# Three vector instructions moved at the hand-over from self-attention to cross-attention, in a fused stack of attention layers

## The chip, the cores and the metric

The kernel runs on one core of a Trainium2 chip. Such a core has a matrix engine (TensorE, PE in the profile, with its weight loads as PEld) and three others that work on vectors: VectorE (DVE), ScalarE (ACT) and GpSimd (POOL). A fifth queue, SyncE (SP), issues transfers. Each engine takes its instructions in the order of its own queue; between engines, semaphores make one wait for another. Matmuls read from the on-chip memory SBUF and write to the accumulators, PSUM, which POOL doesn't use here.

The metric is the device time of one execution in microseconds, as the median of several runs.

## What is computed

Four blocks one after another, on x of shape (8, 256, 128) and a context of shape (8, 64, 64), in float32. The third block is nearly all of the work: six layers, each with self-attention (16 heads of 64, a mask on the keys), cross-attention to the context's 64 rows (16 heads, a mask), and a feed-forward part. Cut to what matters:

```python
def _mha(s, t, kv_w, q_w, o_w, o_b, mask):
    kv = s @ kv_w
    k, v = jnp.split(kv, 2, axis=-1)
    q = t @ q_w
    k, v, q = (_heads(k), _heads(v), _heads(q))
    scores = jnp.einsum('bhqd,bhkd->bhqk', q, k) * D ** (-0.5)
    scores = jnp.where(mask[:, None] == 0, jnp.float32(-1000000000.0), scores)
    attn = jax.nn.softmax(scores, axis=-1)
    o = jnp.einsum('bhqk,bhkd->bhqd', attn, v)
    o = o.transpose(0, 2, 1, 3).reshape(t.shape[0], t.shape[1], H * D)
    return o @ o_w + o_b

def step(t, p):
    skv, sq, sow, sob, ckv, cq, cow, cob, w1, b1, w2, b2, pg, pb = p
    tn = _ln(t, norm_g, norm_b)
    t = _mha(tn, tn, skv, sq, sow, sob, tgt_mask) + t
    tn = _ln(t, norm_g, norm_b)
    t = _mha(src, tn, ckv, cq, cow, cob, src_mask) + t
    tn = _ln(t, pg, pb)
    t = t + (jax.nn.relu(tn @ w1 + b1) @ w2 + b2)
    return (t, None)
```

Two smaller attention blocks come ahead of the six layers and one behind them.

## The kernel before

**An order written by hand.** The program is laid out in *ticks*. `at(tick, phase, fn)` (L304) puts a step down; at the end the steps are run sorted by tick and then by phase, and each engine's instructions are chained in just that order (L1338 to L1348). So the phase of a step is its place in the queue of every engine that it uses; a step with instructions on ACT, DVE and POOL takes a place in all three. Transfers (SP) aren't chained. Between engines only data and free buffers make an instruction wait.

**A layer.** Self-attention (`plan_sa`) takes four ticks a batch, for eight batches; cross-attention (`plan_ca`) then takes two ticks a batch, one for each tile of 128 query rows (`qt`). With `T_ca` as the first tick of cross-attention, the hand-over is:

- tick `T_ca - 2`, phase 3.7: `keys_both` makes the keys of batches 0 and 1 (matmuls L1138, copies to SBUF on ACT, L1144).
- tick `T_ca - 1`: the last two score tiles of self-attention (batch 7). `scores` (L946, PE), `exps` (L960 on DVE: mask, minimum and copy out of PSUM; L965 on ACT: exponential and its sum), `divide` (reciprocal L973 on DVE, four scalings L975 on POOL), `turn` (two 32 x 32 block transposes L985 on DVE). The first tile's `divide` is at phase 2.3 and its `turn` at 8.1; the second's `divide` is at 8.0 and its `turn` at phase 2.2 of tick `T_ca`. At phase 3.0 stand the attention sums of the first half of the heads (`values(0)`, L1001), whose two PSUM tiles are copied out by L309 (DVE) and L311 (ACT). At phase 6 stand the next batch's moments for the layer norm (L856 to L862, DVE).
- tick `T_ca`: `scores` of cross-attention for batch 0, first query tile (L366, PE, phase 1), and `lower` (phase 2): the copy out of PSUM (L377, ACT), the maximum of each row and head (L379, DVE), its subtraction (L380, POOL). At phase 8 the exponential (L386, ACT).
- tick `T_ca + 1`: the same for the second query tile; `divide` of the first (sums L390 and reciprocal L391 on DVE, scaling L392 on POOL) at phase 2.4; `values(1)`, the attention sums that need the last `turn`, at phase 3.0 (L1001, copies L309 and L311).
- tick `T_ca + 2`: `scores` for batch 1 (L366), a pair of transposes (L889), the output projection of batch 7's self-attention (L1019), the context's values for batch 0 (L328, copied by L334 on ACT), the keys of batches 2 and 3 (L1138).

**The mask of the context's keys.** `mask_keys` (L1150) adds a row of the mask to the last 32 partitions of a batch's keys, in place: one instruction of 32 x 1024 elements with two inputs in SBUF (L1152). Queries have a constant in their last row, so the scores get the mask with the matmul. It stands at phase 1.9 of tick `T - 1` for even batches and `T - 2` for odd ones, where `T` is the batch's first tick: for batch 0 that is `T_ca - 1`, for batch 1 it is `T_ca`, ahead of `lower`.

**PSUM.** One pool of four tiles of two banks serves every matmul in turn, so a tile is written again only when the fourth one back has been copied out. The tile of L1019 is the one that L309 empties for `values(1)`.

Of the kernel before, what the change touches and what calls it, by code (L numbers as in the profile page):

```python
# [27 lines left out]
def tile_xattn_stack(ctx: ExitStack, tc: tile.TileContext, io, out: bass.AP):  # L28
    nc = tc.nc
# [15 lines left out]
    def two_banks(base):  # L45
        return psum.tile([P, 1024], F32, tag="ps", name=uniq(base))
# [10 lines left out]
    def big(tag, bufs=4, shape=(P, 1024), dtype=F32):  # L57

        return heap.tile(list(shape), dtype, tag=tag, name=uniq(tag), bufs=bufs)
# [244 lines left out]
    def at(tick, phase, fn):  # L304
        plan.setdefault(tick, []).append((phase, fn))
# [7 lines left out]
    def residual(b, bias):  # L313
        tb = sb([P, QT, D], "tb", 3)
        nc.gpsimd.tensor_tensor(
            tb, tt(b), bias.unsqueeze(1).to_broadcast([P, QT, D]), ALU.add
        )
        return tb

    def values_of(b, wvo):  # L320

        ps = two_banks("mm").rearrange("p (r k x) -> p r k x", r=2, k=2)
        w = wvo.rearrange("p (g a) d -> p a g d", g=2)
        for k in range(2):
            for a in range(4):
                for r in range(2):
                    rows = slice(r * DM, (r + 1) * DM)
                    nc.tensor.matmul(  # L328
                        ps[32 * a : 32 * a + 32, r, k, :],
                        lhsT=ctx2[rows, b, 32 * k : 32 * k + 32],  # L330
                        rhs=w[rows, a], start=True, stop=True,
                    )
        vw = big("v", shape=(P, 2, 2, 2, D))
        nc.scalar.copy(  # L334
            vw.rearrange("p r k g d -> p (r k g d)"), ps.rearrange("p r k x -> p (r k x)")
        )
        return vw

    def plan_weights_64(tick, qt, qT, keys, values, halves, take):

# [95 lines left out]
            take(ps)  # L438

        at(tick, 1, scores)  # L440
        at(tick, 2, lower)
        if halves:
            at(tick + 1, 2.05, exps)
            at(tick + 1, 2.5, turn)
# [245 lines left out]
    def plan_l0(b, T):  # L690
# [88 lines left out]
        for qt in range(QT):  # L779
            plan_weights_64(  # L780
                T + qt, qt, lambda: st["q"], lambda: st["k"], lambda: st["VW"], True,
                lambda ps, qt=qt: add(qt, ps),
            )
# [342 lines left out]
    def plan_ca(l, b, T):  # L1126
        st = {}
        fold = W["fold", l]

        def keys_both():  # L1130

            res = [big("q", shape=(D, 4, 4, M)) for _ in range(2)]
            for g in range(2):
                ps = two_banks("mm").rearrange("p (r a x) -> p r a x", r=2, a=4)
                for a in range(4):
                    for r in range(2):
                        rows = slice(r * DM, (r + 1) * DM)
                        nc.tensor.matmul(  # L1138
                            ps[:, r, a, :], lhsT=fold["AT"][rows, 4 * g + a, :],
                            rhs=ctx2[rows, b : b + 2, :].rearrange("p b m -> p (b m)"),  # L1140
                            start=True, stop=True,
                        )
                for i in range(2):
                    nc.scalar.copy(  # L1144
                        res[i][:, :, 2 * g : 2 * g + 2, :].rearrange("p a r k -> p r a k"),
                        ps[:, :, :, i * M : (i + 1) * M],
                    )
            keys_of[b], keys_of[b + 1] = res

        def mask_keys():  # L1150
            last = keys_of[b][96:].rearrange("p a c k -> p (a c) k")
            nc.vector.tensor_tensor(  # L1152
                last, last, nm2[96:, b].unsqueeze(1).to_broadcast([32, 16, M]), ALU.add
            )

        def make_values():
            st["VW"] = values_of(b, fold["WVO"])

        def res():
            st["tb"] = residual(b, W["ca", l][3])  # L1160

        ahead(b, (T - 5, 6), (T - 3, 2.95), (T - 2, 2.9), last_off, last_on, st)
        if b % 2 == 0:
            at(T - 2, 3.7, keys_both)
        at(T - 1 - b % 2, 1.9, mask_keys)
        at(T + 2, 3.2, make_values)
        at(T + 2, 7, res)

        def add(qt, ps):
            nc.vector.tensor_add(t[:, QT * b + qt, :], ps[:, :D], st["tb"][:, qt, :])  # L1170

        for qt in range(QT):
            plan_weights_64(
                T + qt, qt, lambda: st["tT"], lambda: keys_of[b], lambda: st["VW"],
                False, lambda ps, qt=qt: add(qt, ps),
            )

    def plan_ff(l, b, T, T_second, steps=None):
# [117 lines left out]
    for l in range(NL):  # L1296
        T_ca = T0 + 4 * B
        T_next = T_ca + 2 * B
        for b in range(B):
            plan_sa(l, b, T0 + 4 * b)  # L1300
        plan_ca_weights(l, T_ca - 7)
        for b in range(B):
            plan_ca(l, b, T_ca + 2 * b)
            T_ff = T_ca + 2 * b + 7
            if l + 1 < NL:
                plan_ff(l, b, T_ff, T_ff + 2)
            elif b < B - 2:
                plan_ff(l, b, T_ff, T_ff + 1)
            else:

                T_ff -= b - B + 3
                done = T_ca + 2 * b + 4
                plan_ff(
                    l, b, T_ff, T_ff + 1,
                    (4.6, (done, 6), (done, 8.7), (T_ff, 2.9)),
                )
            T_end[b] = T_ff + 1
        if l > 0:
            at(T0 + 8, -1, lambda l=l: load_ff(l))
        if l + 1 < NL:  # L1320
            at(T_ca + 4, -1, lambda l=l: load_sa(l + 1))
            at(T_next + 1, -1, lambda l=l: load_ca(l + 1))
        T0 = T_next
# [82 lines left out]
```

## Time and profile before

| what | us |
|---|---|
| median of 3 runs | 2408.69 (2408.59 to 2411.47) |
| the profiled execution's own time | 2410.73 |
| its span (first to last instruction) | 2409.0 |
| one layer (from one layer's first L1152 to the next's) | 368.6 |
| L1152 on DVE, 48 in all | 1.22 to 1.65 each |
| L379 on DVE, 112 in all | 1.22 each |
| L380 on POOL, 112 in all | 1.90 each |
| L985 on DVE, 768 in all | 0.69 each |
| mean granted TensorE clock | 0.985 |

The page gives for each engine its busy time, its share of the span and its instructions. The chain of work that ended last is followed back from the last instruction, at each step to what released it. A timeline has a line for each run of like instructions: start, time, engine, line, operation, out<-in, shapes, count, and in brackets the idle time before it and what ended it. A table of stretches has, for each, its length, the busy time of an engine with its number of records, the TensorE clock that was granted (1.00 is full), the share of the DMA engines and GB/s. Times within the span count from its start.

On DVE, the hand-over of the first layer begins with the mask of batch 0 at 393.00 us, and the mask of batch 1 runs at 401.63.

### The profile page before, as it was taken

Reading aid. Unit: us, or ns where it says so; the run is one execution under the profiler, and the core shown is the slowest. Engines: PE = TensorE matmul, PEld = TensorE weight load, DVE = VectorE, ACT = ScalarE, POOL = GpSimd, SP = SyncE. Lnnn points to the kernel's source line nnn. Section 1 sums busy time; section 2 is a strip of 40 time slices with the busy share of each in tenths; the row PEclk is TensorE's granted clock in tenths of the full one; section 3 lists DMA queues with packets and bytes.
Section 4 is the critical chain, followed back from the end, with each engine's and each line's share of the span. In section 5 each row is a group of like instructions: output and inputs, shape, how many; then the busy total and the mean of one; then the engine's idle time right before and its main releaser. Section 6 shows DMA issues by size and latency. Waiting matters only on the chain.

```text
span 2409.0 us, 97481 instructions
## 1 busy us (share of the span) xinstructions
PE 2300.7 (96%) x41124; PEld 1696.1 (70%) x41124; DVE 1922.7 (80%) x6269; ACT 1720.0 (71%) x4544; POOL 1398.4 (58%) x2243
## 2 busy tenths in 40 slices
PE   7889999999998999998999999899999899999897
PEld 3557776777776777776677777677777677777675
DVE  5678888967888967888877888877888877888885
ACT  4567777767777677777677778677778668777663
POOL 2445556854555864555865555865555774555774
PEclk9989999999999999999999999999999999999998
DMA  6000012001012001012001012000012000010000
GB/s 180 2 12 15 21 56 65 2 3 30 21 50 60 12 3 30 21 43 68 12 3 30 21 38 71 14 2 18 25 38 73 21 2 18 25 38 12 2 4 16
DMA packets 98932, 70.67 MB, mean 29 GB/s; under 512 B 7936, under 2 KB 93632, under 8 KB 98496
## 3 DMA queue, kind: packets, MB, share of 16 engines
q1 hardware_dynamic: 97904, 64.12, 9.9%
q8 instruction: 323, 5.29, 1.0%
q14 instruction: 113, 0.93, 0.1%
q10 hardware_dynamic: 592, 0.33, 0.1%
HBM read 59.19 MB, written 5.24 MB: 27 GB/s over the span
## 4 chain that ended last, share of the span: by engine, by line
PE 80%; DVE 11%; ACT 6%; issue 1%; POOL 1%; DMA 1%; SPq 0%; ACTq 0%; POOLq 0%; DVEq 0%
PE mm L909 14%; PE sc L946 13%; PE mm L1001 13%; PE mm L1019 7%; PE mm L928 7%; PE mm L434 6%; PE sc L366 4%; PE mm L1203 4%; PE mm L1186 3%; DVE m L379 2%; PE mm L328 2%; DVE e L960 2%; PE tp L889 2%; ACT e L965 1%; PE mm L1138 1%
## 5 line engine op out<-in xcount | busy, mean ns | idle before, releaser
L975 POOL TENSOR_SCALAR e<-e,rs 128x256 f32<-128x256 f32 x1536 | 714.8, 485 | 724.7 <-DVE rs L973 714.8
L965 ACT ACTIVATE e<-e,mn 128x256 f32<-128x256 f32 x1536 | 758.5, 495 | 145.5 <-DVE mn L960 144.6
L960 DVE CUSTOM_DVE_ANT_0 e<-sc,nm 128x256 f32<-128x256 f32 x1536 | 543.4, 419 | 116.7 <-PE sc L946 115.3
L985 DVE STREAM_TRANSPOSE eTc<-e 128x512 f32<-128x512 f32 x768 | 513.8, 693 | 54.0 <-POOL e L975 53.1
L1001 PE MATMUL mm<-eTc,v 32*64 32x256 f32 x12288 | 372.7, 385 | 25.1 <-DVE eTc L985 25.1
L946 PE MATMUL sc<-k,q 64*32 64x256 f32 x12288 | 380.5, 382 | 1.4 <-ACT v L311 0.6
L1001 PEld LDWEIGHTS mm<-eTc,v 32*64 32x64 f32 x12288 | 283.8, 134 | 111.0 <-issue 44.3
L380 POOL TENSOR_TENSOR e<-e,m 128x1024 f32<-128x1024 f32 x112 | 213.1, 1902 | 207.1 <-DVE m L379 206.8
L946 PEld LDWEIGHTS sc<-k,q 64*32 64x32 f32 x12288 | 221.7, 107 | 122.9 <-issue 45.9
L965 ACT ACTIVATION_READ_ACCUMULATOR e<-e,mn 128x1 f32 x1536 | 287.7, 187 | 0.0
L379 DVE TENSOR_REDUCE m<-e 128x16 f32<-128x1024 f32 x112 | 136.4, 1218 | 102.4 <-ACT e L377 100.3
L434 PE MATMUL mm<-v,o 128*128 128x128 f32 x1536 | 192.8, 279 | 18.7 <-DVE o L400 11.5
L434 PEld LDWEIGHTS mm<-v,o 128*128 128x128 f32 x1536 | 178.9, 192 | 41.4 <-issue 26.9
L909 PE MATMUL mm<-tT,w_sk 128*128 128x256 f32 x768 | 189.3, 389 | 0.0
L1019 PEld LDWEIGHTS mm<-w_sow,o 128*128 128x128 f32 x1536 | 175.1, 192 | 19.0 <-issue 12.3
L311 ACT COPY v<-mm 128x1024 f32<-128x1024 f32 x96 | 97.2, 1012 | 124.8 <-PE mm L928 124.8
L1019 PE MATMUL mm<-w_sow,o 128*128 128x128 f32 x1536 | 183.6, 278 | 2.8 <-ACT WVO L1100 2.8
L366 PE MATMUL sc<-q,tT 128*32 128x256 f32 x3072 | 185.5, 382 | 0.3 <-DVE t L1170 0.3
L928 PE MATMUL mm<-w_sv,tT 128*32 128x256 f32 x3072 | 185.6, 382 | 0.0
L392 POOL TENSOR_TENSOR e<-e,r 128x1024 f32<-128x1024 f32 x96 | 182.6, 1902 | 0.5 <-DVE r L391 0.5
L909 PE MATMUL mm<-tT,w_sq 128*128 128x256 f32 x768 | 173.6, 379 | 0.0
L909 PEld LDWEIGHTS mm<-tT,w_sk 128*128 128x128 f32 x768 | 138.2, 190 | 44.2 <-issue 29.2
(226 smaller groups left out, 3457.6 us busy)
## 6 DMA issues: line engine op xcount, KB each, us to landing
nm<-mask_d SPq DMA_DIRECT2D x192, 128.0 KB
w_sk<-in_L_sa_kv_dram SPq DMA_DIRECT2D x6, 512.0 KB
w_sv<-in_L_sa_kv_dram SPq DMA_DIRECT2D x24, 128.0 KB
w_sq<-in_L_sa_q_dram SPq DMA_DIRECT2D x6, 512.0 KB
w_sow<-in_L_sa_ow_dram SPq DMA_DIRECT2D x6, 512.0 KB
w_ckv<-in_L_ca_kv_dram SPq DMA_DIRECT2D x12, 256.0 KB
w_cq<-in_L_ca_q_dram SPq DMA_DIRECT2D x6, 512.0 KB
w_cow<-in_L_ca_ow_dram SPq DMA_DIRECT2D x6, 512.0 KB
```

The lines of the kernel that those rows point to most:

```text
L366: nc.tensor.matmul(sc[32 * a : 32 * a + 32, q, :], lhsT=qT()[:, qb * 32 : (qb + 1) * 32], rhs=keys()[:, a].rearrange("p h k -> p (h k)"), ...
L380: nc.gpsimd.tensor_tensor(e, e, m.unsqueeze(2).to_broadcast([P, 16, M]), ALU.subtract)
L434: nc.tensor.matmul(ps[:, :D], lhsT=eT[:, s].rearrange("p q x -> p (q x)"), rhs=vw[:, r, k, g, :], start=(s == 0), stop=(s == 7),)
L909: nc.tensor.matmul(ps[:, i * S : (i + 1) * S], lhsT=w[:, c * P : (c + 1) * P], rhs=st["tT"], start=True, stop=True,)
L928: nc.tensor.matmul(ps[32 * a : 32 * a + 32, i, :], lhsT=st["tT"][:, kb * 32 : (kb + 1) * 32], rhs=sv[:, a].rearrange("p g x -> p (g x)"), ...
L946: nc.tensor.matmul(sc[32 * a : 32 * a + 32, r, j, :], lhsT=st["q"][g][rows, a, qb * 32 : (qb + 1) * 32], rhs=st["k"][g][rows, a, :], start ...
L960: nc.vector.tensor_tensor_reduce(e[:, i, :], sc4[:, i, :], st["nm"][:, 2 * jj + i % 2, :], -1.0, 3.0 * BIG, ALU.add, ALU.min, mn[:, i : i ...
L965: nc.scalar.activation(e[:, i, :], e[:, i, :], AF.Exp, scale=-1.0, bias=mn[:, i : i + 1], accum_out=rs[:, i : i + 1],)
L975: nc.gpsimd.tensor_scalar(e[:, i, :], e[:, i, :], rs[:, i : i + 1], 1.0, ALU.mult, ALU.mult)
L985: nc.vector.transpose(eT[:, r, :, 2 * jj : 2 * jj + 2, :], e[:, 2 * r : 2 * r + 2, :].rearrange("p j (k x) -> p k j x", x=32),)
L1001: nc.tensor.matmul(ops[a // 2][r * HD : (r + 1) * HD, a % 2, :S], lhsT=st["v"][kb // 4][rows, kb % 4, (2 * g + r) * HD : (2 * g + r + 1) * ...
L1019: nc.tensor.matmul(st["ps"][:, j * D : (j + 1) * D], lhsT=st["oT"][c // 4][:, c % 4, j * P : (j + 1) * P], rhs=sow[:, c, :], start=(c == 0 ...
```

## The change

`mask_keys` of batch 0 is issued on GpSimd, at phase 2.2 of tick `T_ca - 1` and not on VectorE at 1.9. That of batch 1 stays on VectorE and in tick `T_ca`, but moves from phase 1.9 to 5.5. The step `lower` of batch 0's first query tile moves from phase 2 to 2.25 of tick `T_ca`, which puts its three instructions behind the turning at 2.2. All other batches keep their places.

In the queues, for each of the six layers: POOL gets L1152 between the eight scalings L975 that were there and the next four. VectorE loses L1152 ahead of the last two score tiles. Further on, its order was L1152, L379, two L985, L379 and becomes two L985, L379, L1152, L379. TensorE's, ScalarE's and SyncE's orders stay as they were.

```diff
-    def plan_weights_64(tick, qt, qT, keys, values, halves, take):
+    def plan_weights_64(tick, qt, qT, keys, values, halves, take, lower_at=2):
...
         at(tick, 1, scores)
-        at(tick, 2, lower)
+        at(tick, lower_at, lower)
...
         def mask_keys():
             last = keys_of[b][96:].rearrange("p a c k -> p (a c) k")
-            nc.vector.tensor_tensor(
+            (nc.vector if b else nc.gpsimd).tensor_tensor(
                 last, last, nm2[96:, b].unsqueeze(1).to_broadcast([32, 16, M]), ALU.add
             )
...
         if b % 2 == 0:
             at(T - 2, 3.7, keys_both)
-        at(T - 1 - b % 2, 1.9, mask_keys)
+
+        at(T - 1 - b % 2, {0: 2.2, 1: 5.5}.get(b, 1.9), mask_keys)
         at(T + 2, 3.2, make_values)
...
             plan_weights_64(
                 T + qt, qt, lambda: st["tT"], lambda: keys_of[b], lambda: st["VW"],
                 False, lambda ps, qt=qt: add(qt, ps),
+                2.25 if b == 0 and qt == 0 else 2,
             )
```

## The prediction

> **What bounds the kernel now.** First the page's busy times and its chain of work that ended last:
>
> ```profile
> PE 2300.7 (96%) x41124; PEld 1696.1 (70%) x41124; DVE 1922.7 (80%) x6269; ACT 1720.0 (71%) x4544; POOL 1398.4 (58%) x2243
> PE 80%; DVE 11%; ACT 6%; issue 1%; POOL 1%; DMA 1%; SPq 0%; ACTq 0%; POOLq 0%; DVEq 0%
> ```
>
> TensorE sets the end nearly everywhere, so time is to be had only where it waits. The change acts once in each of six layers, where self-attention hands over to cross-attention. The first mask L1152 starts at 393.0, 761.6, 1130.1, 1498.7, 1867.2 and 2235.8 us, with the same neighbours each time, so I work out the first layer and multiply by six. The chain in order of time (start, us, what):
>
> ```profile
> 393.00 1.23 DVE q L1152
> ...
> 401.63 1.33 DVE q L1152
> 403.00 1.22 DVE m L379
> 404.21 0.63 DVE eTc L985
> ...
> 404.98 5.89 PE mm L1001 x128
> ```
>
> All that the change moves stands on it: the first batch's mask (393.00), the second's (401.63), the first maximum (403.00). Behind them is the turning L985, and behind that TensorE, idle for 3.11 us. L1001 then takes 5.89 us, where the same 128 records took 3.70 at 394.06. About 0.5 of the excess is the wait for the second half of the turning (it ends at 405.42); the rest is the clock (stretches: us, PE busy, granted clock, DMA):
>
> ```profile
> 402.59:406.00 3.41, 1.02 (x23) 1.00 0.00 0
> 406.00:409.41 3.41, 3.41 (x78) 0.50 0.02 5
> ...
> 429.89:433.30 3.41, 1.85 (x30) 1.00 0.00 0
> 433.30:436.72 3.42, 3.40 (x45) 1.00 0.02 5
> ...
> 160.24:163.65 3.41, 1.73 (x14) 1.00 0.01 2
> 163.65:167.07 3.42, 2.95 (x50) 0.50 0.02 5
> ```
>
> The half clock comes in stretches of 3.413 us, or two in a row, on one grid through the run. With that grid laid over PE's records, from 95 to 2390 us each full-clock stretch with 1.69 us of idle or more is followed by a half one, and none with 1.56 or less (at the start and end, with other matmuls, three of 0.96 to 1.33 are). I take 1.6 as the border. A half stretch costs 3.41/2 = 1.7 us of matmul work.
>
> **The change, step by step.** *First mask on GpSimd.* The trace has no such instruction there. From below its price is four L975 (256 columns each, 0.453 apart): 1.8 us; from above L380, two inputs and 1024 columns a partition: 1.9, plus 1.33 if a VectorE mask's worth of blocking fell on it. I take 1.9, the same form. It starts behind POOL's last L975 (393.6) and the key copies L1144 (393.45) and ends at 395.6. POOL's next work waits for L973, which now comes at about 397.6; the scores L366 that need the keys start at 397.70. So 2.1 us are to spare in POOL's idle stretch, and either price costs nothing; without that cover L366 would be late by the excess.
>
> On VectorE 1.23 us go. The next L960 then waits for the first half of L946, whose last record ends at 393.45, plus the 0.11 that L960 stands behind its scores (median of 119 waits): 393.56 for 394.25. The copy L309 also needs the first tile of L1001 (397.55): 397.66 for 398.29, so **0.63 earlier** from there through the moments to the second L973 (399.62 for 400.25).
>
> *Second mask and first maximum behind the last turning.* Both lay between 401.60 and 404.13 on VectorE. With them gone the turning waits for the last L975, in POOL's timeline
>
> ```profile
> 400.51 2.80 POOL L975 TENSOR_SCALAR e<-e,rs 128x256 f32<-128x256 f32 x4 [0.19 <-DVE rs L973]
> 404.29 1.90 POOL L380 TENSOR_TENSOR e<-e,m 128x1024 f32<-128x1024 f32 x1
> ```
>
> The four take 2.80 and not 1.85, because the fourth takes 1.44 for 0.48: it ends 0.35 behind the end of L1152, which ran beside it. That goes too, so they run from 399.87 to 401.71; L985 follows its L975 by 0.03 and takes 0.68: it ends at 402.42 for 405.42, **3.0 earlier**. TensorE, busy until 401.87 as before, then waits some 0.6 and not 3.5, with no half clock there: L1001 ends at 402.49 + 3.66 = 406.15 for 410.87, and L366 behind it at 408.0.
>
> *What is late next.* TensorE's next large work, L1019, needs L309's copy, which frees its PSUM tile; in VectorE's queue that stands behind the second query tile's maximum and the first one's sums:
>
> ```profile
> 408.22 1.22 DVE L379 TENSOR_REDUCE m<-e 128x16 f32<-128x1024 f32 x1 [2.79 <-ACT e L377]
> 409.35 1.21 DVE L390 TENSOR_REDUCE r<-e 128x16 f32<-128x1024 f32 x1
> 410.60 0.25 DVE L391 RECIPROCAL r<-r 128x16 f32<-128x16 f32 x1
> 410.90 0.69 DVE L309 COPY o<-mm 128x512 f32<-128x512 f32 x1
> ```
>
> These hang on the chain L379, L380 (POOL), L386 and L377 (ACT), L379. Its head starts at 402.37 for 403.00. But the order of the changed kernel puts the second mask straight behind that L379, at 403.6, just as POOL gets to L380, 1.30 behind L379's start (403.67; the same 1.30 at 408.22 and 413.85). What happens when the two meet, on VectorE and on POOL elsewhere:
>
> ```profile
> 477.52 1.53 DVE L1152 TENSOR_TENSOR q<-q,nm 32x1024 f32<-32x1024 f32 x1
> ```
> ```profile
> 477.94 1.71 POOL L315 TENSOR_TENSOR tb<-t,w_fb 128x256 f32<-128x256 f32 x1
> ```
>
> L315 takes 0.72 elsewhere; here it ends 0.60 behind the mask's end. So whichever starts second is held until the first is done, and POOL then needs its own time less 0.12. L1152 starts at once behind L379 (0.03 to 0.04 behind its neighbour's end at 401.63), POOL only after a semaphore, 0.08 behind it. At 2327.26 a lead of 0.02 was enough for L1152 to run its 1.22 unhindered while POOL's L290 was held to 1.29. So I take the mask as first: it ends at 404.8 and L380 at 404.8 + 1.78 = 406.6, for 406.19. The gain of 0.63 is a **loss of 0.4** here, and L386, L377, L379, L390, L391 follow: L309 starts at 411.25, ends at 411.92, and L1019 starts at 412.0 for 412.94: **0.95 earlier**, all that is left of 4.7. If POOL comes first, L380 ends at 405.57 and L1019 starts at 411.0: 1.95 earlier. These are the ends.
>
> *The clock again.* TensorE is now idle from 408.0 to 409.0 (L889 waits for L875), some 0.2 between its two transposes, and from 409.75 to 412.0: 3.4 in all. However the grid lies over it, one stretch has 1.6 or more. So the half clock isn't gone; it falls on L1019 and L328, which run without a break to 417.7. It costs 1.7 where it begins behind 412.0 and down to 0.8 where it begins at 410.2; over all places about 1.4.
>
> Sum of a layer: -0.95 + 1.4 = +0.5 (from -0.1 to +0.75); of six: +3.0 (-0.6 to +4.5). The profiled span is 2409.0 and its run 2410.73, so that one would become 2413.7. The median, 2408.69, lies 2.0 below, and the runs shown go up to 2411.47; a layer is 368.57 us and 108 grid steps are 368.64, so a run keeps one place of the grid in all six layers, and the runs may differ by that. I add the 3.0 to the median: **2411.7 us**.
>
> The Trainium skill ("TensorE: Matmul & The Clock Gate", Part 1 and its closing table) has the clock drop only after a wholly idle window of about 3.4 us and advises against idle gaps above about 3 us; by it, no gap of 1.0 to 2.3 us would cost the clock, and the sum would be six times -0.95. This case's rows at 160.24 and 402.59 contradict it, with 1.7 and 2.4 us of idle.
>
> **The rivals.** *POOL's L380 comes first* (15%). For it: the lead is only 0.05. Idle is 2.7 us and a sixth of the grid's places avoid the half clock: mean cost 1.2, so -0.75 a layer, 2408.69 - 4.5 = 2404.2.
>
> *The clock stays full in the forecast's order* (8%): the border lies higher for broken idle than for one gap. Then -0.95 a layer, 2403.0.
>
> *Slower: two half stretches in a row* (15%). Place: the idle from 408.0 to 412.0. If a grid line cuts it so that both sides hold 1.6 or more (3.4 allows it, for some 0.4 of 3.41 us; a later L309 widens that quickly, and then L1019 to L1138 all run at half), a layer costs 2.7 in place of 1.4, and with the 0.95 gives +1.8: 2419.5 if in all six, 2415 if in three or four. It decides from 3.2 us of idle on.
>
> **How the numbers follow.** The forecast has 62%. Its own range is 2408 to 2415: the six-layer ends on the lowest run and on the profiled one. For 8 in 10 it reaches down to POOL first (2404) and up to some double stretches (2416.5). What measurement can tell from no change is about 0.2%, 4.8 us: faster is below 2403.9, slower above 2413.5. Forecast: 3% faster, 40% same, 19% slower. POOL first: 6% and 9%. Full clock: 6% and 2%. Double stretch: 2% same, 13% slower. Together 15% faster, 53% same, 32% slower.
>
> **What would show it.** L1152 on POOL at 393.6 taking 1.9; L985's end some 3.0 earlier and L1001 at about 3.7 in all layers; L1152 on VectorE directly before a late L380 (some 2.9 recorded, held) with L386 0.4 later; PE idle before L1019; the half-clock stretches still six or more, now over L1019. I am wrong if L380 shows 1.9 there, if L1019 follows L889 without a gap, if the clock is full across the hand-over, or if POOL's mask reaches past 397.6 and L366 waits for it.

## The result, and the profile after

The changed kernel takes 2415.78 us in the median of 13 runs (2410.36 to 2418.08), the kernel before 2409.1 beside it (2406.28 to 2412.77, 13 runs). The ratio is 1.0019, with a 95% interval of 1.0011 to 1.0026: slower by 2.6 to 6.3 us, some 4.6 us in the middle. The forecast was 2411.7, 3.0 us more than before, in a range from 2404.0 to 2416.5.

The profiled run of the changed kernel was the lowest of the 13, and its span of 2408.7 is no longer than before. That isn't the layers' doing: from the first instruction to the first L1138 of the first hand-over it took 387.76 us (before 390.19), and from the last such L1138 to the end 174.41 (before 176.02). From the first to the last such L1138, five layers, it took 1846.48 for 1842.81. So the layers are what must be compared, and I count times at the hand-over from **the layer's first L1138** (the keys of batches 0 and 1) on.

The chain of what ended last, in order of time, in the changed kernel's first layer (start, us, what; L1138 starts at 387.76):

```profile
396.90 0.02 issue
396.92 0.18 DVE ve L859
397.10 0.06 DVE mneg L862
397.16 0.09 DVE rs L973
397.25 0.08 issue
397.34 1.85 POOL e L975 x4
399.19 0.02 issue
399.21 0.71 DVE eTc L985
399.92 1.11 DVE m L379
401.03 0.07 issue
401.10 2.95 POOL e L380
404.05 0.02 issue
404.07 0.02 ACT e L386
...
408.69 0.55 DVE o L309
409.25 0.04 issue
409.29 5.47 PE mm L1019 x32
```

No mask is on the chain any more, and L975's four take 1.85 and not 2.80. What stands there instead is L380 with 2.95 (before 1.90, and not on the chain), and L1019 with 5.47 (before 3.74). The two moved masks, the work that they meet on GpSimd and the copy L309, from the timelines of POOL and DVE:

```profile
391.26 2.38 POOL L1152 TENSOR_TENSOR q<-q,nm 32x1024 f32<-32x1024 f32 x1
395.24 1.84 POOL L975 TENSOR_SCALAR e<-e,rs 128x256 f32<-128x256 f32 x4 [1.60 <-DVE rs L973]
401.10 2.94 POOL L380 TENSOR_TENSOR e<-e,m 128x1024 f32<-128x1024 f32 x1 [0.99 <-DVE m L379]
```
```profile
401.05 1.22 DVE L1152 TENSOR_TENSOR q<-q,nm 32x1024 f32<-32x1024 f32 x1
408.61 0.63 DVE L309 COPY o<-mm 128x512 f32<-128x512 f32 x1
```

In the kernel before, TensorE's timeline had L1019 and L328 like this (L1138 at 390.19):

```profile
412.94 3.74 PE L1019 MATMUL mm<-w_sow,o 128*128 128x128 f32 x32
416.61 1.09 PE L328 MATMUL mm<-WVO,ctx 64*32 64x256 f32 x32
```

In the changed one, TensorE's timeline, in the first layer and in the third, and the clock in stretches of its grid in the first, the second and the third:

```profile
399.37 4.31 PE L1001 MATMUL mm<-eTc,v 32*64 32x256 f32 x128
403.61 1.93 PE L366 MATMUL sc<-q,tT 128*32 128x256 f32 x32
406.47 0.71 PE L889 MATMUL tp<-ident,xn 128*128 128x128 f32 x2 [0.92 <-ACT xn L875]
409.29 5.47 PE L1019 MATMUL mm<-w_sow,o 128*128 128x128 f32 x32 [2.10 <-DVE o L309]
```
```profile
1147.25 6.79 PE L1019 MATMUL mm<-w_sow,o 128*128 128x128 f32 x32 [2.11 <-DVE o L309]
```
```profile
405.96:409.37 3.41, 0.74 (x3) 1.00 0.00 0
409.37:412.78 3.41, 3.41 (x16) 0.50 0.02 5
774.60:778.01 3.41, 0.66 (x3) 1.00 0.00 0
778.01:781.42 3.41, 3.07 (x14) 0.50 0.00 0
781.42:784.84 3.42, 3.42 (x56) 1.00 0.10 28
1143.24:1146.65 3.41, 0.93 (x10) 1.00 0.00 0
1146.65:1150.06 3.41, 2.81 (x13) 0.50 0.00 0
1150.06:1153.48 3.42, 3.42 (x18) 0.50 0.07 19
```

The wait ahead of L1001 (3.11 us before) is gone, and with it the half clock there. A wait of 2.10 us for L309 has come ahead of L1019, and the half clock now falls on L1019. A half stretch is one stretch of the grid at half clock: there is one in five of the layers and there are two in the third. In the third, TensorE was idle for 2.48 us of the stretch ahead, and for another 0.60 of the first half stretch before L1019 began; a second half stretch followed. In the second layer the first half stretch was idle for 0.34 only, and none followed.

Where the gain and the loss lie, counted from L1138:

| | L1001 ends | L1019 starts | L328 starts | half stretches |
|---|---|---|---|---|
| before, all six layers | 20.68 | 22.75 | 26.42 | one, on L1001 |
| changed, layers 1, 4, 5, 6 | 15.92 | 21.53 | 26.92 | one, on L1019 |
| changed, layer 2 | 15.92 | 21.53 | 26.75 | one, on L1019 |
| changed, layer 3 | 15.92 | 21.53 | 28.25 | two, on L1019 |

L328 closes the hand-over. It comes 0.5, 0.33 and 1.83 later, 4.2 us over six layers.

### The profile page after: what moved, and what is told of

Same layout as the page of the kernel before. It is cut to its first block, busy times and chain, and to the rows that moved or that the text cites. A ratio compares the mean times of both kernels' runs of the same rounds, so it can differ in the third digit from the quotient of the medians.

```text
span 2408.7 us, 97499 instructions
## 1 busy us (share of the span) xinstructions
PE 2299.1 (95%) x41124; PEld 1700.2 (71%) x41124; DVE 1913.8 (79%) x6263; ACT 1719.8 (71%) x4544; POOL 1406.9 (58%) x2249
## 4 chain that ended last, share of the span: by engine, by line
PE 80%; DVE 10%; ACT 6%; POOL 2%; issue 1%; DMA 1%; SPq 0%; ACTq 0%; POOLq 0%; DVEq 0%
PE sc L946 14%; PE mm L909 14%; PE mm L1001 13%; PE mm L1019 8%; PE mm L928 7%; PE mm L434 6%; PE sc L366 4%; PE mm L1205 3%; PE mm L1188 3%; DVE m L379 2%; PE mm L328 2%; PE mm L1138 1%; ACT e L965 1%; PE tp L889 1%; DVE r L390 1%
## 5 line engine op out<-in xcount | busy, mean ns | idle before, releaser
L975 POOL TENSOR_SCALAR e<-e,rs 128x256 f32<-128x256 f32 x1536 | 703.2, 478 | 710.2 <-DVE rs L973 700.3
L985 DVE STREAM_TRANSPOSE eTc<-e 128x512 f32<-128x512 f32 x768 | 513.8, 693 | 55.0 <-POOL e L975 54.1
L1001 PE MATMUL mm<-eTc,v 32*64 32x256 f32 x12288 | 362.7, 378 | 6.8 <-DVE eTc L985 6.8
L380 POOL TENSOR_TENSOR e<-e,m 128x1024 f32<-128x1024 f32 x112 | 219.2, 1958 | 214.4 <-DVE m L379 214.4
L1001 PEld LDWEIGHTS mm<-eTc,v 32*64 32x64 f32 x12288 | 277.0, 131 | 88.7 <-issue 27.2
L379 DVE TENSOR_REDUCE m<-e 128x16 f32<-128x1024 f32 x112 | 136.2, 1216 | 105.6 <-ACT e L377 103.2
L434 PE MATMUL mm<-v,o 128*128 128x128 f32 x1536 | 192.9, 279 | 18.7 <-DVE o L400 11.5
L1019 PE MATMUL mm<-w_sow,o 128*128 128x128 f32 x1536 | 195.2, 289 | 15.4 <-DVE o L309 12.6
L1019 PEld LDWEIGHTS mm<-w_sow,o 128*128 128x128 f32 x1536 | 186.0, 202 | 32.8 <-DVE o L309 13.8
L434 PEld LDWEIGHTS mm<-v,o 128*128 128x128 f32 x1536 | 178.9, 192 | 41.4 <-issue 26.9
L311 ACT COPY v<-mm 128x1024 f32<-128x1024 f32 x96 | 97.2, 1013 | 124.4 <-PE mm L928 124.4
L366 PE MATMUL sc<-q,tT 128*32 128x256 f32 x3072 | 185.5, 382 | 0.3 <-DVE t L1171 0.3
L392 POOL TENSOR_TENSOR e<-e,r 128x1024 f32<-128x1024 f32 x96 | 182.7, 1903 | 0.5 <-DVE r L391 0.5
L386 ACT ACTIVATE e<-e 128x1024 f32<-128x1024 f32 x112 | 119.0, 1063 | 81.4 <-POOL e L380 81.4
```

Source lines behind the costliest of these rows:

```text
L366: nc.tensor.matmul(sc[32 * a : 32 * a + 32, q, :], lhsT=qT()[:, qb * 32 : (qb + 1) * 32], rhs=keys()[:, a].rearrange("p h k -> p (h k)"), ...
L380: nc.gpsimd.tensor_tensor(e, e, m.unsqueeze(2).to_broadcast([P, 16, M]), ALU.subtract)
L434: nc.tensor.matmul(ps[:, :D], lhsT=eT[:, s].rearrange("p q x -> p (q x)"), rhs=vw[:, r, k, g, :], start=(s == 0), stop=(s == 7),)
L975: nc.gpsimd.tensor_scalar(e[:, i, :], e[:, i, :], rs[:, i : i + 1], 1.0, ALU.mult, ALU.mult)
L985: nc.vector.transpose(eT[:, r, :, 2 * jj : 2 * jj + 2, :], e[:, 2 * r : 2 * r + 2, :].rearrange("p j (k x) -> p k j x", x=32),)
L1001: nc.tensor.matmul(ops[a // 2][r * HD : (r + 1) * HD, a % 2, :S], lhsT=st["v"][kb // 4][rows, kb % 4, (2 * g + r) * HD : (2 * g + r + 1) * ...
```

## The experiments

The theory at this point: (1) the mask on GpSimd is hidden; (2) the second mask on VectorE holds L380, and by way of L386, L379 and L390 the copy L309; (3) L1019 can't start before L309, whatever L1001 gains; (4) the idle stretch that is left brings the half clock onto L1019. All ratios are against the kernel before, run beside; each diff is against the changed kernel.

**The first mask alone.**

```diff
-        at(T - 1 - b % 2, {0: 2.2, 1: 5.5}.get(b, 1.9), mask_keys)
+        at(T - 1 - b % 2, 2.2 if b == 0 else 1.9, mask_keys)
...
-                2.25 if b == 0 and qt == 0 else 2,
```

> Times of the hand-over count from the layer's first keys matmul L1138: before, L1019 starts at 22.75 and the next group L328 at 26.42; after, 21.53 and 26.92 (28.25 where two half stretches meet). Only the first mask goes to GpSimd, the second mask and the first maximum stay where they were. If the forecast's steps hold: the mask on POOL is hidden (it took 2.38 in after, in an idle stretch), L960 comes 0.69 and L309 0.63 earlier, the half stretch still lies on L1001, L1019 starts at 22.1 and L328 at 25.8: 0.6 a layer, 3 to 4 us faster than before, ratio about 0.9985. Rival, the loss of after comes from the mask on GpSimd (its 2.38 us): L366 late behind it, L328 at 26.4 or later, not faster than before.

Measured: 2402.32 us, ratio 0.9965 (0.9953 to 0.9978): faster than both kernels. L1019 starts at 22.01 and L328 at 25.68 in three layers with a half stretch on L1001, so 0.74 a layer, as expected (in a fourth the stretch came sooner, and L328 at 25.32). In two of the six layers none fell there (L1001's wait is 2.37 and not 3.11 now), and L328 came at 24.3. That makes the total larger than expected: 3 x 0.74, one layer of 1.10, 2 x 2.1, together 7.6. The mask on GpSimd isn't the loss; the rival falls.

**The other two moves alone.**

```diff
-            (nc.vector if b else nc.gpsimd).tensor_tensor(
+            nc.vector.tensor_tensor(
...
-        at(T - 1 - b % 2, {0: 2.2, 1: 5.5}.get(b, 1.9), mask_keys)
+        at(T - 1 - b % 2, 5.5 if b == 1 else 1.9, mask_keys)
```

> The first mask is back on VectorE in its old place; the second mask and the first maximum are moved as in the changed kernel. Counted from the layer's first L1138. If the forecast's steps hold: L985 ends some 2.4 earlier than before and L1001 with it, L380 is held again (2.9 recorded), L386 comes 1.0 later than before, L1019 starts at 22.4 (before 22.75), and the half stretch falls on L1019: L328 at 27.4 to 27.6, later where two half stretches meet. 1.0 us a layer and more, ratio 1.003 to 1.005. Rival, the first mask makes the loss: L328 at or below 26.4, ratio 1.000 or less.

Measured: 2423.08 us, ratio 1.0043 (1.0030 to 1.0055). POOL's timeline has the held L380, and TensorE's the late and slow L1019 (the first L1138 at 393.17):

```profile
407.24 2.94 POOL L380 TENSOR_TENSOR e<-e,m 128x1024 f32<-128x1024 f32 x1 [0.99 <-DVE m L379]
```
```profile
415.43 5.47 PE L1019 MATMUL mm<-w_sow,o 128*128 128x128 f32 x32 [2.10 <-DVE o L309]
```

L1019 starts at 22.27. L328 comes at 27.66 in three layers, and at 28.7 to 28.9 in the three others, which have two half stretches. So the loss of the changed kernel is made by the two moves behind the turning, and the first mask pays a part of it back.

**What holds L380.** Batch 1's mask instruction is left out.

```diff
-        at(T - 1 - b % 2, {0: 2.2, 1: 5.5}.get(b, 1.9), mask_keys)
+        if b != 1:
+            at(T - 1 - b % 2, 2.2 if b == 0 else 1.9, mask_keys)
```

> The changed kernel without batch 1's mask instruction (that addition is left out of the computation), so that nothing on VectorE stands beside L380. If the shared port is what holds L380: L380 takes 1.90, L386 comes 1.05 earlier than in after, L1019 starts at 20.5 from the layer's first L1138 (after 21.53), idle before it about 2; the half stretch still falls on L1019 in most layers, L328 at 25.3 to 25.9 there and at 24.2 where it doesn't. Against before 3 to 8 us faster, ratio 0.997 to 0.999. Rival, L380 is late for another reason: L380 stays near 2.9, L1019 at 21.5, time as after.

Measured: 2404.41 us, ratio 0.9975 (0.9963 to 0.9986). POOL's timeline, first layer (L1138 at 393.20):

```profile
406.54 1.90 POOL L380 TENSOR_TENSOR e<-e,m 128x1024 f32<-128x1024 f32 x1 [0.99 <-DVE m L379]
```

L380 takes 1.90 again, with the same wait for L379 ahead of it, and L1019 starts at 20.49, 1.04 earlier, which is what the hold had cost. In three layers a half stretch still fell on L1019 (L328 at 25.89), in three none (24.26). So the mask beside it is shown to be what holds L380; that the idle time that is left can still bring the half clock is shown too.

**The clock by itself.** TensorE gets work for the idle stretch ahead of L1019, and nothing else changes.

```diff
+            for _ in range(fill):
+                nc.tensor.transpose(ps[:, S : S + P], ident, ident)
...
+            fill=16 if b == 2 else 0,
```

> The changed kernel with 16 more TensorE transposes of the identity, into a part of the PSUM tile that nobody reads, behind the two of L889 ahead of L1019: 1.75 us of TensorE work in the idle stretch of 2.1 us before L1019. If the half clock over L1019 eats the gain: no half stretch at the hand-over, L1019 starts at 21.5 as in after but takes 3.74 and not 5.3 to 6.8, L328 at 25.2 from the layer's first L1138: 1.7 a layer and more better than after, 1.2 better than before, 6 to 8 us faster than before, ratio about 0.997, and the runs lie closer together than those of after. Rival, the clock isn't what costs (the late L309 alone, or the transposes only add work): L328 at 26.9 or later, ratio 1.002 or more.

Measured: 2406.25 us, ratio 0.9978 (0.9969 to 0.9987). TensorE's timeline, first layer (L1138's line is L1140 in this kernel, at 392.84, and L1019's is L1021):

```profile
412.09 1.91 PE L891 MATMUL tp<-ident 128*128 128x128 f32 x16
414.36 3.84 PE L1021 MATMUL mm<-w_sow,o 128*128 128x128 f32 x32 [0.36 <-DVE o L309]
```

L1019 starts at 21.53 in every layer, as in the changed kernel, and takes 3.84; no half stretch falls on any hand-over, L328 comes at 25.3 in all six, and a layer takes 367.44 for 368.57 before. (Without the filler's records each of the six hand-overs of this trace would have a stretch busy for only 0.8 to 1.4 us; with them the least there is 2.4.) So with late L309 and all, the change would have won 1.1 us a layer, had the clock stayed full: the half clock over L1019 turns a gain into a loss. The runs spread over 6.4 us (2400.84 to 2407.23), hardly less than the changed kernel's 7.7: that part of the expectation was wrong, and the spread doesn't come from the hand-overs alone.

**L309's place in VectorE's queue** (called the run with the sums early below).

```diff
-        at(T + 5, 3.0, lambda: values(1))
+        at(T + 5, 1.5 if b == B - 1 else 3.0, lambda: values(1))
```

> The changed kernel, with the attention sums of the last batch's second half (L1001 and the copies L309 and L311) at phase 1.5 of their tick and not 3.0: L309 then stands ahead of the second maximum on VectorE, L311 ahead of the second copy L377 on ScalarE; TensorE's order is as before. Counted from the layer's first L1138. If it is L309's place in VectorE's queue that holds L1019 (after: 21.53): L309 starts at 15.8, L1019 follows L889 at 19.5 to 19.7, TensorE is idle 1.4 before L889 and no half stretch falls on L1019, L328 at 23.3 (after 26.92 to 28.25, before 26.42). 3 us a layer better than before: 16 to 20 us, ratio 0.992 to 0.9935. Rival, L1019 hangs on something else (the held L380 by way of L386 and L311): L1019 at 21 or later, ratio 0.999 or more.

Measured: 2397.73 us, ratio 0.9950 (0.9937 to 0.9962). TensorE's timeline, first layer (L1138 at 392.42):

```profile
411.63 0.71 PE L889 MATMUL tp<-ident,xn 128*128 128x128 f32 x2 [1.41 <-ACT xn L875]
412.18 3.74 PE L1019 MATMUL mm<-w_sow,o 128*128 128x128 f32 x32
...
426.09 2.02 PE L434 MATMUL mm<-v,o 128*128 128x128 f32 x16 [1.02 <-DVE o L400]
```

L1019 starts at 19.76 behind L889 without a wait, no half stretch falls on a hand-over, and L328 comes at 23.43, 3.0 earlier than before. So it was L309's place. The total is less than expected: a layer takes 366.32, 2.25 less than before. The rest is given back at L434, which waits 1.02 us for L400 (0.36 before). L400 turns the weights of cross-attention on VectorE, and in that queue the mask of batch 2 stands ahead of it. This mask now comes while L392 runs on GpSimd (POOL's and DVE's timelines):

```profile
419.72 1.90 POOL L392 TENSOR_TENSOR e<-e,r 128x1024 f32<-128x1024 f32 x1
420.58 2.13 DVE L1152 TENSOR_TENSOR q<-q,nm 32x1024 f32<-32x1024 f32 x1
```

Before, it took 1.22 at 420.44, behind 2.49 us of idle time. Here it ends 1.09 behind L392, takes 0.91 more in all six layers, and is on the chain that leads to L400. That this is what L434 waits for is read from the chain; no run takes it away alone.

**The transposes L889 behind L1019 as well.**

```diff
-            ahead(b, (T - 5, 6), (T - 3, 2.95), (T - 2, 2.9), last_off, last_on, st)
+            ahead(
+                b, (T - 5, 6), (T - 3, 2.95), (T - 2, 3.15 if b == 2 else 2.9), last_off, last_on, st
+            )
```

> As the run with the sums early, and the pair of transposes L889 of the third batch behind L1019 and not ahead of it. L1019 then waits only for L366 (17.8) and for the PSUM tile that the copy L377 empties (18.75): L1019 at 18.8, no half stretch, L328 at 22.6. 3.8 us a layer better than before: 21 to 24 us, ratio 0.990 to 0.9915. If the transposes set something behind (the third batch's scores come late): less than the run with the sums early.

Measured: 2398.24 us, ratio 0.9950 (0.9936 to 0.9963), a layer 366.32. L1019 starts at 17.74 and L328 at 21.72, both earlier than expected, and it gains nothing: L1138 now waits 1.24 us for L377, and L434 the same 1.02 for L400, with the mask of batch 2 held to 2.13 again. The hand-over's end no longer sets the layer.

**The changed kernel again.** The same kernel, for a second profile.

> The changed kernel, unaltered, for a second profile. The first one's run was the lowest of 13 and had one double half stretch in six layers. If the number of double half stretches is what makes its runs spread (2410 to 2418): two or three doubles here, each 1.3 to 1.8 us, and a time near 2415; L1019 starts at 21.53 in every layer. If the spread comes from elsewhere: one double or none and a time near 2415 all the same.

Measured: 2413.90 us, ratio 1.0015 (1.0006 to 1.0024). L1019 starts at 21.55 in all layers; one layer, the third again, has two half stretches; from the first L1138 to the last it is 1846.78, with L328's 0.5 in the last layer some 4.4 us more than before. So the layers cost the same in both profiles, 4.2 and 4.4, and the ratios of both sets of runs say 3.6 and 4.6. The profiled spans differ by 3.2 (2411.9 and 2408.7): ahead of the first hand-over by 3.9 (391.69 and 387.76), less 0.7 behind it. Two or three double stretches had been expected if these made the spread; there was one in each profile, so between these two they don't. Both profiles began at nearly the same place of the grid, though (the first half stretch at 21.61 and 21.64), so they don't say how many doubles the other runs have.

What does go with the spread is the clock of the whole run. Among the first 13 runs it was 0.986 in the two shortest (2410.36 and 2411.0) and 0.983 in the six longest (2415.94 to 2418.08). A half stretch is 0.0007 of a run's clock, so 0.003 is some four of them; at up to 1.7 us each that would be, by estimate, up to 7 us of a spread of 7.7. Ahead of the first L1138 the shortest profiled start (387.76) has 8 half stretches, those of 390.2 to 392.5 have 10 or 11, and those of 392.4 to 393.2 have 12. Why their number differs from run to run stays open.

**Only L309 early, then the mask behind it.** On top of the run with the sums early, first L311 goes back to its old place:

```diff
-            for i in range(2):
-                copy_to(oT[:, 2 * i : 2 * i + 2, :], ops[i][:, :, :S], i == 0)
+            copies = [
+                lambda i=i: copy_to(oT[:, 2 * i : 2 * i + 2, :], ops[i][:, :, :S], i == 0)
+                for i in range(2)
+            ]
+            copies[0]()
+            if g and b == B - 1:
+                st["copy"] = copies[1]
+            else:
+                copies[1]()
...
-        at(T + 5, 3.0, lambda: values(1))
+        at(T + 5, 1.5 if b == B - 1 else 3.0, lambda: values(1))
+        if b == B - 1:
+            at(T + 5, 3.0, lambda: st.pop("copy")())
```

> As the run with the sums early, but ScalarE's copy L311 stays at its old place behind L875 (phase 3.0): only L309 comes early. Counted from the layer's first L1138. If L311's 0.55 us on ScalarE ahead of L377 and L875 is what kept L889 at 19.2 there: L377, L875 and L889 come 0.5 earlier, L1019 at 19.2, L328 at 22.9 to 23.0 (with the sums early 23.43), the second query tile's chain 0.5 earlier too, a layer 365.8 to 366.0 us for 366.32; 1.5 to 3 us better, ratio about 0.994. Rival, the layer is set behind the hand-over (L434 waits for L400): a layer stays at 366.3.

Measured: 2400.76 us, ratio 0.9955 (0.9942 to 0.9967). L1019 at 19.26 and L328 at 22.93, as expected; but a layer takes 366.7. The 0.5 was given back, and more: the second L366 of batch 1 now waits 1.67 us for the addition that frees its PSUM tile, which stands behind L400 on VectorE. So the rival held in that something behind the hand-over sets the layer; it is this wait, though, and not L434's (0.25 there), and the layer is 0.4 longer than the rival said.

Then, on top of that, the second mask moves behind L309:

```diff
-        at(T - 1 - b % 2, {0: 2.2, 1: 5.5}.get(b, 1.9), mask_keys)
+        if b == 1:
+            at(T - 1, 1.6, mask_keys)
+        else:
+            at(T - 1 - b % 2, 2.2 if b == 0 else 1.9, mask_keys)
```

> As the run before, and the second mask behind L309 on VectorE and not beside L380. If the held L380 is what now limits the layer by way of L386, L390, L392 and L400: L380 takes 1.90, the chain behind it comes 1.0 earlier, L366 for batch 1 waits for the mask until 17.7 and TensorE is idle 1.8 before it, L1019 at 20.0, L328 at 23.7 (25.4 where a half stretch falls there), yet a layer no longer than 366 where none does. If TensorE's order still limits: a layer 0.5 to 1 longer than in the run before.

Measured: 2398.15 us, ratio 0.9943 (0.9930 to 0.9957). L380 takes 1.90, L328 comes at 23.83, and a layer 366.3 where no half stretch falls: the same as with the sums early, by the other trade. TensorE's new wait of 2.10 us ahead of L366 brings the half clock back in three of the six layers (L328 at 25.4 to 25.7). The trace puts that wait down to L875, which ends at 409.0, and the mask ends at 408.87; in the run just above, L366 began ahead of L875, and only the mask was moved since, so I take it as the mask's. Among the four versions with the sums early the intervals overlap, so none is shown to be the best; all are faster than both kernels.

## Why the prediction was right, and where its sizes were off

- **The first mask is hidden on GpSimd: right**, though its price was not. It took 2.38 us, above the 1.8 and 1.9 of the nearest rows; its end at 393.64 still left 1.6 us to POOL's next work at 395.24.
- **L985 3.0 us earlier, L1001 with it, no half clock there: right.** L1001 ends at 15.92 behind L1138; the forecast's 406.15 is 15.96 on that count.
- **The mask comes first, and L380 is held: right.** It stands in the profile with 2.94 from 401.10, the mask with 1.22 from 401.05. Without that mask L380 took 1.90.
- **L1019 hangs on L309, so that little is left of 4.7 us: right**, shown by putting L309 ahead. The forecast had L1019 at 21.8 (0.95 earlier); it came at 21.53, 1.22 earlier.
- **The half clock falls on L1019: right, and mis-sized.** The forecast took "about 1.4" us for it, as a mean over all places of the grid. From L1019's start to L328 it took 1.55 to 1.73 more than before in five of the six layers, where the half stretch began between 0.33 ahead of L1019 and 1.06 behind it, and 3.05 in the third. (0.1 of each isn't the clock's: behind a wait L1019 takes 3.84 and not 3.74 at full clock too, as in the run with the filler.) That is 1.9 in the mean; less the 1.22 it makes +0.7 a layer, where the forecast said +0.5, and 4.2 us in six layers where it said 3.0. So the two errors, 0.27 earlier and 0.5 dearer, cancel in part. By the medians the result lies above the forecast's own range of 2408 to 2415, and inside the whole one by 0.7 us, thanks to what was added there for double stretches.
- **Two half stretches in a row** was a rival of its own there, at +1.8 for a layer that has it. One layer in six had it, at +1.83, in both profiles. Two things were wrong with it. The forecast asked for 1.6 us of idle on both sides of the grid line; on the second side, that is within the first half stretch, much less was enough. Another half stretch followed where that one was idle for 0.60 (changed kernel), 0.66 (its second profile) and 0.78 to 1.16 (three layers of the other two moves alone); none did at 0.34 and 0.38. So the low end of the forecast's price, 0.8 us for a half stretch that begins 1.8 ahead of L1019, can't be had: by these rows a second one follows there. And the forecast let a run keep one place of the grid in all six layers, which fits the kernel before (the half stretch begins 15.81 to 16.20 behind L1138); the changed layer of 369.05 is 0.41 longer than 108 grid steps, so its hand-over moves over the grid and can meet the place of two. With one such layer, 1.3 more, the sum would have been +4.3; that is worked out afterwards.
- **The border of the clock was put at 1.6 us of idle; in the six layers it lies higher, near 1.9.** Without the second mask the idle was cut by L889:

```profile
1511.57:1514.98 3.41, 1.28 (x13) 1.00 0.00 0
1514.98:1518.39 3.41, 3.41 (x19) 0.50 0.01 3
2248.85:2252.26 3.41, 1.55 (x13) 1.00 0.00 0
2252.26:2255.68 3.42, 3.42 (x55) 1.00 0.00 0
```

  With the first mask alone, and with the mask behind the copy, it was one gap:

```profile
1871.78:1875.20 3.42, 1.45 (x39) 1.00 0.02 5
1875.20:1878.61 3.41, 3.41 (x78) 0.50 0.00 0
```
```profile
1507.41:1510.82 3.41, 1.51 (x29) 1.00 0.01 2
1510.82:1514.24 3.42, 3.42 (x36) 1.00 0.00 0
```

  Idle for 1.86 (cut) and 1.90 us (one gap) the clock stayed full; idle for 1.97 (one gap) and 2.13 (cut) it didn't. So it isn't the cut that decides, as the forecast's rival had it. The 1.69 of the row at 160.24 lies ahead of the six layers, among other matmuls. It changed no conclusion, as the full-clock stretches ahead of the changed kernel's half stretches were idle for 2.1 us and more.
- The 2411.7 was the median before plus 3.0. The measured ratio puts the changed kernel 4.6 higher, and its layers 4.2 to 4.4. The median of its 13 runs is 6.7 higher; the rest of that isn't traced to a place in the program.

## What to carry to other kernels

A wait taken off the busiest engine is worth what the next wait behind it allows, so follow that engine's queue to the next instruction that needs another engine before adding anything up: here 4.8 us shrank to 1.2 at one copy that stood behind two reductions in VectorE's queue, and moving that copy turned a loss of some 4.6 us into a gain of some 12. Where idle time moves, ask what the TensorE clock does behind its new place; work with no purpose in the gap showed it in one run. And where a VectorE instruction with two inputs in SBUF meets GpSimd's work, ask which of the two the path hangs on: here the mask cost L380 1.04 us, and once the hand-over was shorter, L392 cost the next mask 0.91.

## What the runs showed of the hardware that was not expected

- The 32 x 1024 mask takes 2.38 us on GpSimd in each of the six layers and in every run that had it, a quarter more than L380's 1.90, with a quarter of the partitions, as many elements in each and two inputs as well. No VectorE instruction with two SBUF inputs ran beside it. Why it is slower stays open.
- A lead of 0.05 us (401.05 and 401.10) was enough for the mask to run its 1.22 while L380 was held for 1.04 us, in all six layers of each of the seven profiles with that order. With the sums early, where L392 had a lead of 0.86 us, it was the mask that was held, by 0.91.
- In the six layers 0.60 us of idle time within a half stretch was enough for another half stretch, while 1.90 us in a stretch at full clock was not enough for a first one.
- What lies outside the hand-overs differs from run to run by about as much as the change makes: up to the first L1138 it took 387.8 to 393.2 us in these profiles, a stretch that the edits don't touch and in which 8 to 12 half stretches fall, and from the last L328 to the end 149.6 in the kernel before and 147.5 and 146.5 in the two profiles of the changed one.
